# A cross-network kernel on one core: another order of the first loads and shifts, and another way to add up the last eight samples

## The chip, the cores and the metric

The kernel runs on one core of one Trainium2 chip. The metric is the device time of one execution in microseconds (us). Before the change the median of three runs is 484.85 us (484.78 to 485.05). Profiled times below are counted from the start of the profiled span, which is 482.9 us long.

## The reference

For 1024 samples, each of F = 64 fields with E = 16 values, three "cross" layers are computed. Each multiplies every field of x with every row of the layer's input h, value by value over e, and mixes the 64 x (rows of h) products to 128 outputs. Of the first two layers one half of the outputs goes to the result and the other half is the next h.

```python
x0 = x; h = x; xs = []
for i in range(3):
    z = jnp.einsum('bfe,bge->bfge', x0, h)          # products of pairs
    z = z.reshape(Bn, f0 * fh, e)
    y = jnp.einsum('oc,bce->boe', Ws[i], z) + bs[i][None, :, None]
    if i != 2:
        x_i, h = y[:, :64, :], y[:, 64:, :]
    else:
        x_i, h = y, y
    xs.append(x_i)
pooled = jnp.sum(jnp.concatenate(xs, axis=1), axis=2)   # sum over e
return pooled @ fc_w.T + fc_b                            # one number for each sample
```

As only a weighted sum over the outputs is wanted, the kernel folds the last layers into a quadratic form: what is left at the end is, for each sample, a sum over 128 rows and over e of products `uu`, and a constant.

## The kernel before

Samples are worked on in 32 chunks of 32; a chunk has N = 32 * 16 = 512 columns. `xa` holds a chunk's fields on 128 partitions (partition p is field p mod 64, so both halves of the rows hold the same data) in four slices, each turned by one field. `xb` holds four other turns. For most chunks both are loaded; for the first two chunks (numbers 2 and 3, called c0 and c1) the turns are made by matmuls with a shift matrix[...]. VectorE (and for some pieces GpSimd) makes the products `z`, TensorE contracts them with `w_all`.

The start: dummy matmuls, the constants' load on ACT's queue, the first loads on SP's queue, the first shifts.

```python
    vs = const_tile("vs", [128, NV])
    nc.scalar.dma_start(out=vs, in_=vec)
    ...
    fv2 = const_tile("fv2", [128, 32])
    nc.scalar.copy(fv2, fc2.to_broadcast([128, 32]))      # fc2 is a column of vs
    ...
    misc = ps.tile([128, N], F32, tag="acc", name="misc", bufs=4)
    zeros = nc.const_aps.tensor(0.0, [128, 128])
    for n in (128,) * 6 + (64,):
        nc.tensor.matmul(misc[:, 0:n], zeros, zeros[:, 0:n], start=True, stop=True)
    ...  # load_xa, load_xb
    c0, c1, c2, c3 = HEAD                                 # 2, 3, 0, 1
    load_xa(c0, slice(0, 1))
    nc.sync.dma_start(out=w0t[:, 0, :], in_=wh)           # weight block 0
    load_xa(c0, slice(1, 2))
    load_xa(c0, slice(2, 4))
    load_xa(c1, slice(0, 1))
    nc.sync.dma_start(out=w0t[:, 1:NJ, :], in_=w0r)       # weight blocks 1 to 3
    load_xa(c1, slice(1, 4))
    ...
    def shift_pair(c, js):
        for r, j in enumerate(js):                        # shift j reads rows halves[r]
            for h in range(2):
                at = 4 * (j + 1) + 16 * h
                nc.tensor.matmul(
                    xbs[c][j][halves[h]], shift[halves[r], at : at + F],
                    xas[c][halves[r], 0, :], start=True, stop=True,
                )

    for j, tag in enumerate(("y", "y", "set", "acc")):
        shifted(c0, j, tag)                               # takes a PSUM buffer of that tag
    shift_pair(c0, (0, 1))
    shift_pair(c0, (2, 3))
```

The first chunk's products and contraction. `h1_weights(j)` adds the two halves of weight block j on VectorE; one half is copied to PSUM by ACT first. The products of shift 1 are GpSimd's, from a copy that ACT makes, as is product 3 of c1.

```python
    nc.scalar.copy(w0o[0], w0s[0][:, :, 1, :])
    h1_weights(0, w0o[0])
    nc.scalar.copy(xb_gps[:, 0, :], xbs[c0][1])
    xbs[c0][1] = xb_gps[:, 0, :]
    for i in ((0, 2), (2, 3), (3, 4)):
        product(c0, 1, *i, engine=nc.gpsimd)
    product(c0, 0, 0, 1)
    product(c0, 0, 1, 2)
    product(c0, 0, 2, NI)
    nc.scalar.copy(w0o[1], w0s[1][:, :, 1, :])
    product(c0, 2, 0, 2)
    h1_weights(1, w0o[1])
    product(c0, 2, 2, NI)
    ...  # the same for weight blocks 2 and 3
    half_contract(c0, 0)

    for j, tag in ((0, "y"), (3, "acc"), (1, "y"), (2, "set")):
        shifted(c1, j, tag)
    shift_pair(c1, (0, 3))
    half_contract(c0, 1)
    shift_pair(c1, (1, 2))
    ...
    product(c0, 3)
    load_chunk(c3)
    half_contract(c0, 2, 3, last=3)
```

Later, `head_q` contracts the same products with further weights (the q part), which go through DRAM (`md`, read back as `ms`) and are added on VectorE.

The end. The last chunk is contracted in two pieces: 24 samples, then the last 8 (`CUT` is 24). `factors` makes `uu` of a piece (ACT copies one factor, VectorE multiplies), `sums` adds it up over e on VectorE, `pool` over the rows with a matmul whose weights are ones, and `finish` adds the constant `cst` and stores.

```python
    first, last = slice(0, CUT), slice(CUT, CB)
    factors(NCH - 1)
    sums(NP - 1, slice(64, 128), slice(0, 1), first)
    for j in range(NJ):
        contract(NCH - 1, j, 1)
    factors(NCH - 1, slice(1, 2))
    sums(NP - 1, slice(64, 128), slice(0, 1), last)
    pool(NP - 1, NP, start=False, stop=True)
    finish(NP - 1, NP, nc.sync, nc.vector)
```

Of the kernel before, what the change touches and what calls it, by code (L numbers as in the profile page):

```python
# [37 lines left out]
F32 = mybir.dt.float32  # L38
AF = mybir.ActivationFunctionType
ALU = mybir.AluOpType  # L40
AX = mybir.AxisListType

F = 64
E = 16
B = 1024
CB = 32
N = CB * E
H2 = N // 2
CUT = 24
NCH = B // CB  # L50
NI = 4
NJ = 4
NT = NI * NJ
XR = 128 + NI
# [10 lines left out]
def cin_kernel(ctx, tc, xra, xrb, wh, w0r, w1h, w2t, wx1, wx0, vec, out):  # L65
    nc = tc.nc
# [6 lines left out]
    ps = ctx.enter_context(tc.tile_pool(name="ps", bufs=2, space=bass.MemoryType.PSUM))  # L73
    dr = ctx.enter_context(tc.tile_pool(name="dr", bufs=1, space=bass.MemoryType.DRAM))
    halves = [slice(0, F), slice(F, 128)]

    def const_tile(name, shape):
        return const.tile(shape, F32, tag=name, name=name)
# [10 lines left out]


    vs = const_tile("vs", [128, NV])
    nc.scalar.dma_start(out=vs, in_=vec)
    fc2, bh1, bh2 = vs[:, 0:1], vs[:, 1:2], vs[0:64, 2:3]
    bcol, fcol, fcb = vs[:, 3:5], vs[:, 5:7], vs[:, 7:8]
    w0ds, fcr = vs[:, 8:72], vs[:, 72:200]

    fv2 = const_tile("fv2", [128, 32])
    nc.scalar.copy(fv2, fc2.to_broadcast([128, 32]))

    v0w = const_tile("v0w", [128, 2, F])  # L100
    v1w = const_tile("v1w", [128, 2, F])
# [2 lines left out]


    zeros = nc.const_aps.tensor(0.0, [128, 128])
    for n in (128,) * 6 + (64,):
        nc.tensor.matmul(misc[:, 0:n], zeros, zeros[:, 0:n], start=True, stop=True)  # L108

    shift = const_tile("shift", [128, 96])  # L110
# [1 line left out]
    for base in (0, 64, -64):  # L112
        nc.gpsimd.affine_select(
            out=shift, in_=shift, compare_op=ALU.not_equal, fill=1.0, base=base,
# [3 lines left out]
    ones = const_tile("ones", [128, 2])  # L118
# [9 lines left out]
    res = const_tile("res", [128, 128])  # L128


    xas, xbs, xxs, xrs, sqs = {}, {}, {}, {}, {}

    def load_xa(c, at=slice(0, NI)):
        if c not in xas or at.start == 0:
            xas[c] = xp.tile([128, NI, N], F32, tag="xa", name=f"xa_{c}")
        nc.sync.dma_start(
            out=xas[c][:, at, :],
            in_=bass.AP(
                tensor=xra.tensor, offset=c * XR * N + at.start * N,
                ap=[[N, 128], [1, (at.stop - at.start) * N]],  # L140
            ),
        )

# [25 lines left out]
    def load_chunk(c):  # L169
        load_xa(c)  # L170
        load_xb(c)

    c0, c1, c2, c3 = HEAD
    w0t = z_tile("w0t")
    w2s = [flat_tile(f"w2_{k}") for k in range(2)]
    w1s = set_tile("w1s")
    load_xa(c0, slice(0, 1))
    nc.sync.dma_start(out=w0t[:, 0, :], in_=wh)
    load_xa(c0, slice(1, 2))
    load_xa(c0, slice(2, 4))  # L180
    load_xa(c1, slice(0, 1))
    nc.sync.dma_start(out=w0t[:, 1:NJ, :], in_=w0r)
    load_xa(c1, slice(1, 4))
    w0s = [w0t[:, j, :].rearrange("p (i v g) -> p i v g", v=2, g=F) for j in range(NJ)]
    xb_gps = xp.tile([128, NJ, N], F32, tag="xb", name="xb_gps")
# [14 lines left out]
    def shift_pair(c, js):  # L200
        for r, j in enumerate(js):
# [4 lines that stand above are left out]
                    xas[c][halves[r], 0, :], start=True, stop=True,  # L206
                )

    for j, tag in enumerate(("y", "y", "set", "acc")):
        shifted(c0, j, tag)  # L210
    shift_pair(c0, (0, 1))
    shift_pair(c0, (2, 3))
# [2 lines left out]
    acc = const_tile("acc", [128, 2, NCH // 2, CB])  # L215
    hb = const_tile("hb", [128, NF // 2, N])
    accs, uus, zs, ys, parts = {}, {}, {}, {}, {}
# [26 lines left out]
    def tiles(j):  # L244

        return (1, 2, 3, 0) if j == NJ - 1 else range(NI)
# [42 lines left out]
                    )  # L289


    def half_contract(c, *js, last=None):
        for j in js:
            for i in tiles(j):
                t = j * NI + i
                for n in range(2):
                    nc.tensor.matmul(  # L297
                        accs[c][halves[n]], w_all[:, t, 0:64],
                        zs[c, j][:, i, n * H2 : (n + 1) * H2],
                        start=(t == 0), stop=(j == last and i == tiles(j)[-1]),  # L300
                    )
# [42 lines left out]
    def sums(k, rows=slice(0, 128), of=slice(0, 2), half=slice(0, CB)):  # L344

        nc.vector.tensor_reduce(  # L346
            acc[rows, of, k, half],
            uus[k][rows, of, E * half.start : E * half.stop].rearrange("p k (b e) -> p k b e", e=E),
            AX.X,
            ALU.add,  # L350
        )
# [27 lines left out]
    nc.vector.memset(w0o[3][SQ, 0, :], 0.0)  # L379
    for j in (2, 3):  # L380
        h1_weights(j, w0o[j])
    half_contract(c0, 0)


    for j, tag in ((0, "y"), (3, "acc"), (1, "y"), (2, "set")):
        shifted(c1, j, tag)
    shift_pair(c1, (0, 3))
    half_contract(c0, 1)
    shift_pair(c1, (1, 2))
    new_acc(c1, H2)  # L390
# [2 lines left out]

    product(c0, 3)
    load_chunk(c3)
    half_contract(c0, 2, 3, last=3)
    keep_h1(c0)

# [8 lines left out]
    for n in range(2):  # L407
        pv = ps.tile([128, 512], F32, tag=("set", "y")[n], name=f"pv2_{n}")
        for k in range(4):
            nc.tensor.matmul(  # L410
                pv[32 * k : 32 * k + 32], fv2, w2s[n][:, k * 512 : (k + 1) * 512],
                start=True, stop=True,
# [6 lines left out]
    for h in range(2):  # L419
        at = slice(32 * h, 32 * h + 32)  # L420
# [40 lines left out]
    for half, queue in enumerate((nc.sync, nc.scalar)):  # L461
        queue.dma_start(
            out=m_ap(0, 32 * half, [[row, F], [1, 32 * F]]), in_=m_rows[halves[half]]
# [86 lines left out]
        head_q(0, j)  # L550

    cst = const_tile("cst", [128, 1])
    made = set()

    def load_products(c, other=None):
# [46 lines left out]
    NP = NCH // 2  # L602
    QP = NP // 4
# [7 lines left out]
            tile_position=(0, 32 * g), skip_group_check=True, **flags,  # L611
        )

    def finish(k0, k1, queue, engine=nc.scalar):
        g, at = k0 // QP, slice(k0 % QP, (k1 - 1) % QP + 1)
        rows = slice(32 * g, 32 * g + 2)
        if engine is nc.scalar:
            engine.activation(res[rows, at, :], po[rows, at, :], AF.Identity, bias=cst[rows])
        else:
            engine.tensor_scalar(res[rows, at, :], po[rows, at, :], cst[rows], None, ALU.add)  # L620
        queue.dma_start(out=outs[:, k0:k1, :], in_=res[rows, at, :])


# [1 line left out]
    for s, c in enumerate(order):  # L625
        k, head = c // 2, c in HEAD
        if order[s - 1] in HEAD and not head:
            for n in range(NF // 2):
                x_v0x(n)
            for n in HEAD:  # L630
                factors(n)
                if n % 2:
                    sums(n // 2)
        if 0 < s < len(order) - 2 and s not in (2, 3):
            load_products(*order[s + 2 : s + (4 if s == 6 else 3)])
        if s in (2, 3):

            if s == 2:
                for n in order[4:6]:
                    load_chunk(n)  # L640
                load_shared(0)
            for j in (0, 1) if s == 2 else (2, 3):
                for n in order[4:6]:
                    product(n, j)
        if s == len(HEAD) + 5:

            pc = ps.tile([128, 1], F32, tag="set", name="pc")
            for j in range(2):
                nc.tensor.matmul(  # L649
                    pc, fcol[:, j : j + 1].to_broadcast([128, 128]), bcol[:, j : j + 1],  # L650
                    start=(j == 0), stop=(j == 1),
                )
            nc.scalar.activation(cst, pc, AF.Identity, bias=fcb, scale=float(E))
        if not head:
            if c % 4 < 2:
                new_acc(c)
            if c == NCH - 1:
                factors(c - 1)
                sums(k, of=slice(1, 2))
                sums(k, slice(0, 64), slice(0, 1))  # L660
                done = acc[:, :, 0:k, :]
                nc.vector.tensor_tensor(done[:, 0], done[:, 0], done[:, 1], ALU.add)
                po = ps.tile([128, QP, CB], F32, tag="set", name="po")
            for j in range(NJ):
                contract(c, j)
                if c == NCH - 1 and j == 1:
                    quarters = [(n, min(n + QP, k)) for n in range(0, NP, QP)]
                    for at in quarters:
                        pool(*at, start=True, stop=True)
                    pool(k, NP, 1, start=True, stop=False)  # L670
                    for at in quarters:
                        finish(*at, nc.sync)
        elif c % 2:
            for n in (c - 1, c):
                new_acc(n)
            for j in range(NJ):
                head_q(k, j)
            contract_shared(0)
        if c % 4 == 1 and not head:
            for n in (1, 2):  # L680
                new_acc(c + n)
            contract_shared(c - 1)
        if s == 0:
            v0_weights()
            load_products(order[2], order[3])

        if c == HEAD[0] or c % 4 in (0, 3) and s and order[s - 1] not in HEAD and c < NCH - 1:
            factors(order[s - 1])
            if order[s - 1] % 2:
                sums(order[s - 1] // 2)  # L690
        elif c % 4 == 2 and not head:
            factors(c - 2)
            factors(c - 1)
            x_v0x(k - 1)
            x_v0x(k)
            sums(k - 1)


    first, last = slice(0, CUT), slice(CUT, CB)
    factors(NCH - 1)  # L700
    sums(NP - 1, slice(64, 128), slice(0, 1), first)
    for j in range(NJ):
        contract(NCH - 1, j, 1)
    factors(NCH - 1, slice(1, 2))
    sums(NP - 1, slice(64, 128), slice(0, 1), last)
    pool(NP - 1, NP, start=False, stop=True)
    finish(NP - 1, NP, nc.sync, nc.vector)


# [69 lines left out]
```

## Time and profile before

| what | value |
|---|---|
| median time | 484.85 us |
| profiled span | 482.9 us |
| TensorE clock granted over the span, mean | 1.0 |
| VectorE busy | 369.0 us (76%) |
| GpSimd busy | 15.4 us (3%) |
| data moved | 87.01 MB, mean 180 GB/s |
| TensorE, main contraction (L256) | 387.6 us |
| TensorE, shifts (L204) | 32 records, 3.9 to 12.9 us |
| first store of the result / last store issued | 470.8 / 480.9 us |

In the profile PE is TensorE's matmul side and PEld its weight loads, DVE is VectorE, ACT ScalarE, POOL GpSimd, SP the engine that issues most DMAs. An fp32 matmul leaves two records. A line such as "9.52 0.38 ACT L373 COPY w0p<-w0t" says: start and length in us, engine, source line, operation, written tile and read tile; the bracket after it has the idle time of the engine before it and what ended that. The end of a matmul is modelled, so its start is the better mark.

### The profile page before, as it was taken

To read this page: it belongs to the slowest core of one execution; us is meant where nothing else is said; L and a number is where in the kernel's file an instruction comes from. 1 tells how busy PE (TensorE), PEld (TensorE's weight loads), DVE (VectorE), ACT (ScalarE), POOL (GpSimd) and SP (SyncE) were. 2 spreads that over 40 slices of the span, in tenths; PEclk is the share of its full clock that TensorE was granted. 3 is DMA by queue.
4 is the path that set the end of the run, shared out by engine and by line. 5 is a ranking of instruction groups with operands and counts; after the bars stand their busy time and mean duration, and the time that the engine had idled before them with its cause. 6 is when DMAs were issued, how large, how long until landed. Compare 5 with 4: busy or idle time off the path is not lost.

```text
span 482.9 us, 4412 instructions
## 1 busy us (share of the span) xinstructions
PE 478.2 (99%) x1802; PEld 215.3 (45%) x1802; DVE 369.0 (76%) x228; ACT 66.9 (14%) x141; POOL 15.4 (3%) x16
## 2 busy tenths in 40 slices
PE   8999999999999999999999999999999999999997
PEld 5564344443344444444444444444444444444555
DVE  5993799998899988898877686766878677771321
ACT  3242033011110121002100011001000010000001
POOL 5330000000000000000000000000000000000000
PEclk9999999999999999999999999999999999999999
DMA  8986996662952683587247344473346630000000
GB/s 336 402 277 185 388 375 276 222 213 113 347 233 91 230 281 119 187 271 281 109 159 219 145 174 175 158 212 111 128 174 215 220 138 38 0 1 0 0 1 1
DMA packets 19658, 87.01 MB, mean 180 GB/s; under 512 B 4818, under 2 KB 5490, under 8 KB 10742
## 3 DMA queue, kind: packets, MB, share of 16 engines
q1 hardware_dynamic: 18582, 85.71, 49.0%
q10 hardware_dynamic: 1056, 1.02, 0.8%
q8 instruction: 14, 0.23, 0.2%
q14 instruction: 6, 0.05, 0.0%
HBM read 85.08 MB, written 1.64 MB: 180 GB/s over the span
## 4 chain that ended last, share of the span: by engine, by line
PE 99%; DVE 1%; issue 0%; ACT 0%
PE acc L256 80%; PE acc L297 6%; PE acc L315 6%; PE acc L272 3%; PE acc L285 1%; PE xp L204 1%; PE misc L108 1%; DVE z L234 1%; PE pm L434 0%; PE pv L410 0%; PE y L277 0%; PE po L609 0%; DVE uu L337 0%; PE pc L649 0%; DVE acc L346 0%
## 5 line engine op out<-in xcount | busy, mean ns | idle before, releaser
L256 PE MATMUL acc<-z,w_all 128*128 128x512 f32 (+2 forms) x928 | 387.6, 579 | 0.0
L234 DVE TENSOR_TENSOR z<-xa,xb 128x2048 f32<-128x2048 f32 x124 | 278.4, 2286 | 41.6 <-PE acc L256 35.3
L256 PEld LDWEIGHTS acc<-z,w_all 128*128 128x128 f32 x928 | 173.1, 190 | 213.0 <-issue 205.9
L239 ACT ACTIVATE z<-xa 32x512 f32<-32x512 f32 x34 | 21.3, 626 | 337.5 <-DVE z L234 335.8
L337 DVE SCALAR_TENSOR_TENSOR uu<-acc,vs,q 64x512 f32<-64x512 f32 (+2 forms) x29 | 21.2, 731 | 57.8 <-ACT q L331 57.6
L297 PE MATMUL acc<-z,w_all 128*64 128x256 f32 x256 | 29.1, 382 | 0.5 <-DVE z L234 0.5
L315 PE MATMUL acc<-z,w_all 128*64 128x512 f32 x128 | 27.9, 593 | 0.0
L331 ACT COPY q<-acc 64x512 f32<-64x512 f32 (+2 forms) x33 | 18.7, 566 | 35.9 <-PE acc L256 19.8
L297 PEld LDWEIGHTS acc<-z,w_all 128*64 128x64 f32 x256 | 18.0, 137 | 12.7 <-DVE z L234 2.1
L234 DVE TENSOR_TENSOR z<-xa,xp 128x2048 f32<-128x2048 f32 (+2 forms) x12 | 20.3, 1746 | 0.6 <-PE xp L204 0.6
L346 DVE TENSOR_REDUCE acc<-uu 128x64 f32<-128x1024 f32 (+4 forms) x19 | 20.3, 1073 | 0.3
L315 PEld LDWEIGHTS acc<-z,w_all 128*64 128x64 f32 x128 | 9.1, 137 | 18.0 <-issue 17.1
L277 PE MATMUL y<-xr,v0w 32*64 32x512 f32 x128 | 15.9, 600 | 0.0
L272 PE MATMUL acc<-xr,v1w 32*64 32x512 f32 (+2 forms) x132 | 15.7, 587 | 0.0
L342 DVE SCALAR_TENSOR_TENSOR uu<-y,cx,xx 128x512 f32<-128x512 f32 x16 | 11.3, 746 | 0.2
L234 POOL TENSOR_TENSOR z<-xa,xb_gps 128x512 f32<-128x512 f32 (+2 forms) x4 | 9.4, 2376 | 4.4 <-ACT xb_gps L366 4.4
L272 PEld LDWEIGHTS acc<-xr,v1w 32*64 32x64 f32 x132 | 5.1, 131 | 10.0 <-issue 9.8
L285 PE MATMUL acc<-sq,w_sq 32*64 32x512 f32 (+2 forms) x132 | 8.7, 574 | 0.0
L533 DVE TENSOR_TENSOR w_all<-ms 128x256 f32<-128x256 f32 x4 | 1.6, 423 | 5.1 <-DMA ms<-md 5.1
L167 ACT ACTIVATE sq<-xr 128x512 f32<-128x512 f32 x8 | 5.0, 630 | 3.2 <-DMA xr<-in_xra 3.0
L285 PEld LDWEIGHTS acc<-sq,w_sq 32*64 32x64 f32 x132 | 3.7, 132 | 3.7 <-issue 3.5
L234 POOL TENSOR_TENSOR z<-xa,xb 128x2048 f32<-128x2048 f32 x1 | 4.6, 4584 | 13.4 <-DMA xb<-in_xrb 13.4
(57 smaller groups left out, 67.6 us busy)
## 6 DMA issues: line engine op xcount, KB each, us to landing
xa<-in_xra SPq DMA_DIRECT2D x32, 1024.0 KB, 4.9
xb<-in_xrb SPq DMA_DIRECT2D x31, 1024.0 KB, 7.7
xr<-in_xra SPq DMA_DIRECT2D x32, 128.0 KB, 7.5
xx<-in_xra SPq DMA_DIRECT2D x32, 128.0 KB, 7.6
w<-in_w2t SPq DMA_DIRECT2D x2, 1024.0 KB, 10.7
w1s<-in_w1h SPq DMA_DIRECT2D x1, 1024.0 KB
w1x<-in_wx SPq DMA_DIRECT2D x1, 1024.0 KB
w0x<-in_wx SPq DMA_DIRECT2D x1, 1024.0 KB, 5.5
```

Source lines behind the costliest of these rows:

```text
L234: engine.tensor_tensor(zs[c, j][:, at, :], xas[c][:, at, :], xbs[c][j].unsqueeze(1).to_broadcast([128, last - first, N]), ALU.mult,)
L239: nc.scalar.activation(zs[c, j][SQ, 0, :], xas[c][SQ, 0, :], AF.Square)
L256: nc.tensor.matmul(acc_c, w_all[:, t, w_cols(c)], zs[c, j][:, i, cols], start=(t == 0 and c % 4 < 2), stop=(t == NT - NI and c % 4 >= 2),)
L272: nc.tensor.matmul(acc_c[halves[1 - n]], v1w[at, m], xr[:, cols], start=(m == 0 and c not in ends), stop=False, tile_position=(at.start, 6 ...
L277: nc.tensor.matmul(ys[c // 2][halves[n]], v0w[at, m], xr, start=(m == 0), stop=(m == 1), tile_position=(at.start, 64 * n),)
L285: nc.tensor.matmul(acc_c[halves[n]], w_sq[at, w_cols(c)][:, 64 * n : 64 * n + 64], sqs[first][at, cols], start=h and (first == 0 or c not ...
L297: nc.tensor.matmul(accs[c][halves[n]], w_all[:, t, 0:64], zs[c, j][:, i, n * H2 : (n + 1) * H2], start=(t == 0), stop=(j == last and i == ...
L315: nc.tensor.matmul(accs[c][halves[1 - c % 2]], w_all[:, t, 64:128], zs[c, j][:, i, :], start=(t == 0), stop=False,)
L331: nc.scalar.copy(q[h, cols], acc_c[64 - h.start : 128 - h.start])
L337: nc.vector.scalar_tensor_tensor(uu[:, cols], acc_c[h], bh1[h], q[h, cols], ALU.add, ALU.mult)
L342: nc.vector.scalar_tensor_tensor(uu_tile(k)[:, 1, :], ys[k], cx, xxs[k], ALU.add, ALU.mult)
L346: nc.vector.tensor_reduce(acc[rows, of, k, half], uus[k][rows, of, E * half.start : E * half.stop].rearrange("p k (b e) -> p k b e", e=E), ...
```

## The change

It has two parts. At the start, the first load comes in two halves of 64 rows, the constants `vs` move behind the weights on SP's queue, weight block 1 gets a load of its own, one dummy matmul goes, and the contraction of product 0 is split around the next chunk's first shifts. This is meant to let the first shifts and the first contraction steps begin when their own data is there, and to fill a wait of TensorE with shifts. At the end, the last 8 samples are added up over the 128 rows on TensorE first, the constant's share (`csl`, 1/(128 * 16) of it on each row) with them by a second matmul, and over e by one VectorE reduction from PSUM straight into the stored result. This is meant to take one VectorE step out of the last chain.

```diff
-    nc.scalar.dma_start(out=vs, in_=vec)
...
-    nc.scalar.copy(fv2, fc2.to_broadcast([128, 32]))
...
-    for n in (128,) * 6 + (64,):
+    for n in (128,) * 5 + (64,):
         nc.tensor.matmul(misc[:, 0:n], zeros, zeros[:, 0:n], start=True, stop=True)
...
-    def load_xa(c, at=slice(0, NI)):
+    def load_xa(c, at=slice(0, NI), rows=slice(0, 128)):
...
-    load_xa(c0, slice(0, 1))
+    for rows in halves:
+        load_xa(c0, slice(0, 1), rows)
     nc.sync.dma_start(out=w0t[:, 0, :], in_=wh)
     load_xa(c0, slice(1, 2))
     load_xa(c0, slice(2, 4))
     load_xa(c1, slice(0, 1))
-    nc.sync.dma_start(out=w0t[:, 1:NJ, :], in_=w0r)
+    for at in (slice(0, 1), slice(1, NJ - 1)):
+        nc.sync.dma_start(out=w0t[:, at.start + 1 : at.stop + 1, :], in_=w0r[:, at])
+    nc.sync.dma_start(out=vs, in_=vec)
     load_xa(c1, slice(1, 4))
...
-    for j, tag in enumerate(("y", "y", "set", "acc")):
+    for j, tag in ((1, "y"), (0, "y"), (2, "set"), (3, "acc")):
         shifted(c0, j, tag)
...
-    half_contract(c0, 0)
+    half_contract(c0, 0, at=(0, 1))
...
     shift_pair(c1, (0, 3))
+    half_contract(c0, 0, at=(2, 3))
     half_contract(c0, 1)
...
     load_chunk(c3)
+    nc.scalar.copy(fv2, fc2.to_broadcast([128, 32]))
     half_contract(c0, 2, 3, last=3)
...
+    csl = const_tile("csl", [128, 1])
+    nc.gpsimd.memset(acc[64:128, 0, NCH // 2 - 1, CUT:], 0.0)
...
             nc.scalar.activation(cst, pc, AF.Identity, bias=fcb, scale=float(E))
+            nc.scalar.activation(csl, cst, AF.Identity, scale=1.0 / (128 * E))
...
-    first, last = slice(0, CUT), slice(CUT, CB)
+    first, last = slice(0, CUT), slice(E * CUT, N)
     factors(NCH - 1)
     sums(NP - 1, slice(64, 128), slice(0, 1), first)
     for j in range(NJ):
         contract(NCH - 1, j, 1)
     factors(NCH - 1, slice(1, 2))
-    sums(NP - 1, slice(64, 128), slice(0, 1), last)
     pool(NP - 1, NP, start=False, stop=True)
-    finish(NP - 1, NP, nc.sync, nc.vector)
+    pl = ps.tile([1, N - E * CUT], F32, tag="acc", name="pl", bufs=4)
+    uu = uus[NP - 1]
+    nc.tensor.matmul(pl, ones[:, 1:2], uu[:, 1, last], start=True, stop=False)
+    nc.tensor.matmul(
+        pl, csl, nc.const_aps.tensor(1.0, [128, N - E * CUT]), start=False, stop=False
+    )
+    nc.tensor.matmul(pl, ones[:, 1:2], uu[:, 0, last], start=False, stop=True)
+    rows, (even, odd) = slice(96, 98), (outs[0:1, NP - 1], outs[1:2, NP - 1])
+    nc.scalar.activation(
+        res[rows, QP - 1], po[rows, QP - 1], AF.Identity, bias=cst[rows]
+    )
+    nc.sync.dma_start(out=even, in_=res[96:97, QP - 1])
+    nc.sync.dma_start(out=odd[:, first], in_=res[97:98, QP - 1, first])
+    rl = hb[0:1, 0, 0 : CB - CUT]
+    nc.vector.tensor_reduce(rl, pl.rearrange("p (b e) -> p b e", e=E), AX.X, ALU.add)
+    nc.sync.dma_start(out=odd[:, CUT:], in_=rl)
```

## The prediction

> **What bounds the kernel now.** I read the page first (busy times, slices, the chain that ended last), then the chain of waits at both ends of the run, then the timeline of the first 13 us, the DMA issues of the first microsecond, and transfer rates by stage.
>
> The page's busy times:
>
> ```profile
> PE 478.2 (99%) x1802; PEld 215.3 (45%) x1802; DVE 369.0 (76%) x228; ACT 66.9 (14%) x141; POOL 15.4 (3%) x16
> ```
>
> TensorE is busy 99% of the span, and the chain is 99% PE. Neither the middle's loads nor VectorE can give much; the change touches only the first 13 us and the last 4. The chain of waits at the start (start us, us, what):
>
> ```profile
> 0.79 3.22 PE misc L108 x14
> 4.00 1.87 PE xp L204 x8
> 5.87 0.02 issue
> 5.90 2.42 DVE z L234 x3
> 8.32 0.04 issue
> 8.37 1.08 PE acc L297 x8
> 9.45 1.02 PE xp L204 x8
> ```
>
> Dummy matmuls (`misc`), first shifts (`xp`), three VectorE products, half the first contraction, the next chunk's shifts. At 5.90 to 8.32 PE waits on VectorE: a contraction step of two 128x256 matmul pairs is 0.43 us (1.08 us for 8 records, less the tail), so of 8.37 minus 7.24 (start of the second step) about 0.7 us is empty. How that goes on, in the timeline of 8.9 to 10.6 us:
>
> ```profile
> 6.68 4.84 POOL L234 TENSOR_TENSOR z<-xa,xb_gps 128x1024 f32<-128x1024 f32 x3 [4.42 <-ACT xb_gps L366]
> ...
> 9.52 0.38 ACT L373 COPY w0p<-w0t 128x256 f32<-128x256 f32 x1 [2.98 <-DVE z L234]
> ...
> 9.93 0.42 DVE L354 TENSOR_TENSOR w_all<-w0t,w0p 128x256 f32<-128x256 f32 x1 [0.49 <-ACT w0p L373]
> ...
> 10.46 0.23 PEld L297 LDWEIGHTS acc<-z,w_all 128*64 128x64 f32 x4 [0.88 <-POOL z L234]
> ```
>
> GpSimd makes product 1 of the first chunk in three pieces, 6.68 to 11.52. ACT copies the second weight block only at 9.52; the named releaser (`z` on DVE) is no operand of that copy, but `w0t` is, so I take it for the 768 KB load of `w0r`. The combined weights are ready at 10.35 and PE goes on at 10.46. First DMA issues, KB, median us to landing:
>
> ```profile
> xa<-in_xra SPq DMA_DIRECT2D x1, 256.0 KB, 3.0
> vs<-in_vec ACTq DMA_DIRECT2D x1, 100.0 KB, 3.2
> ```
>
> xa is issued at 0.74, lands near 3.79, and the first shift starts at 3.94: the load ends last there, not the dummies, whose last record starts at 3.58. Two 1 us windows (busy per engine, clock, DMA share, GB/s), with loads of 128 rows and then loads of 64 and 32 rows under way:
>
> ```profile
> 3.40:4.40 1.00, 1.00 (x8) 0.72 (x10) 0.00 (x0) 0.22 (x1) 0.00 (x0) 1.00 1.06 408
> 61.00:62.00 1.00, 1.00 (x3) 0.38 (x2) 1.00 (x1) 0.16 (x1) 0.00 (x0) 1.00 0.86 213
> ```
>
> A load of fewer rows runs at about half the rate. The end, in the timeline:
>
> ```profile
> 479.55 0.36 DVE L337 SCALAR_TENSOR_TENSOR uu<-acc,vs,q 64x128 f32<-64x128 f32 x1 [2.15 <-ACT q L331]
> 479.94 0.28 DVE L346 TENSOR_REDUCE acc<-uu 64x8 f32<-64x128 f32 x1
> 480.34 0.12 PEld L609 LDWEIGHTS po<-acc,ones 128*2 128x2 f32 x2 [1.31 <-ACT q L331]
> 480.37 0.22 PE L609 MATMUL po<-acc,ones 128*2 128x32 f32 x2 [1.15 <-DVE acc L346]
> 480.63 0.26 DVE L620 TENSOR_SCALAR res<-po,cst 2x32 f32<-2x32 f32 x1 [0.40 <-PE po L609]
> 480.92 0.25 SPq L621 DMA_DIRECT2D out<-res  x1
> ```
>
> A serial tail: product, sum over e, sum over rows, add the constant, store.
>
> **What the Trainium skill says.** "TensorE: Matmul & The Clock Gate", Part 1: the array starts at half clock and is released after a busy window of about 3.4 us, which is free-running, so the moment varies. The trace agrees: eight shift records take 1.75 us from 3.94 (two groups of four, 0.85 us each), and the next eight 0.86 us from 5.68. "SBUF — State Buffer", Door 1: 64 partitions reach only 8 of 16 DMA ports, half the rate; 213 against 408 GB/s above agrees. "DMA: Bandwidth & Descriptors", Anatomy of one DMA: a fixed cost near 2 us, mostly completion; so halving a load cannot halve its 3.0 us. "VectorE: DVE Perf Modes", errata section: an fp32 tensor_tensor takes (N+151)/0.96 ns; for N = 512 that is 691, the trace has 684. The fixed part means a reduction of 128 values (0.28 us here) hardly depends on how many rows it has.
>
> **The change, part by part.**
>
> *One dummy fewer.* The last of the records starts at 3.58, after 6.25 units of 128 columns: about 0.45 us each. PE is free at about 3.26 instead of 3.7. It is worth nothing alone, as the load lands at 3.79.
>
> *First load in two halves, `vs` later.* Before, 262 KB of xa and 102 KB of vs interleave: at 400 GB/s 0.91 us. The first half is 131 KB at 213 GB/s, 0.62 us, so it lands about 0.3 to 0.4 earlier, 3.45. Shift 0 reads only this half: start 3.45 + 0.14 = 3.6, end 1.75 later (cold) at 5.35, product on VectorE at 5.35 + 0.22 (before, 5.68 to 5.90) = 5.55 or so instead of 5.90: gain 0.35. (The first weights, ready at 5.26 before, allow that.) The second half is issued 0.48 us later and its 0.62 us follows the first's: I expect 3.85, as late as all of xa before. Shift 1 reads it and feeds ACT's copy and GpSimd, so GpSimd gains 0.05, perhaps 0.3 if the halves overlap.
>
> *Half of contraction 0 before the next chunk's shifts, half after; other order of the two y buffers.* The shifts (0.86 us and two gaps of 0.14) move into the 0.7 us hole, and their y buffer comes from ACT's early copy. PE finishes contraction 0 and shifts at about 9.4 instead of 10.3. xa of the next chunk has to be there by 7.5; it has 1.57 MB with what comes before it, at 400 GB/s from 2.6 on 6.6, plus 0.4: 7.0.
>
> *`w0r` in two loads.* The second block alone ends at 1.83 MB, about 7.7 instead of some 9.5. The combination no longer waits 0.49 us for ACT; VectorE does it after its 0.35 earlier products, at 9.05, ready at 9.45 instead of 10.35. So contraction 1 could start at 9.55 instead of 10.49.
>
> *What then ends last: GpSimd.* Its third piece is done at 11.52 less 0.05 to 0.3; the last step takes 0.1 latency and 0.43: contraction 1 ends at 11.75 to 12.0 instead of 12.24. PE has been handed 0.9 us there and waits for most of it. Front gain 0.2 to 0.5, I take 0.3.
>
> *Does it stay?* TensorE has no other hole up to 41.7 us. The tightest later point is the second weight block of the q part: its VectorE addition ends at 44.05, PE wants it at 41.70 + 16 records of 0.215 = 45.1: slack 1.05. The first product after that waits for xb until 51.6 and is done at 53.9, wanted at 55.5: slack 1.6. A gain of 0.3 fits in both even if these loads don't move.
>
> *The tail.* Removed: reduction 0.28 plus 0.03, the 0.22 us row sum, the add 0.26. Added after the product (ends 479.91): a row sum of 128 columns. Start 0.15 later as before, 480.06; second record 0.11 later, 0.275 long: 480.45. Then a reduction of 1x128 from PSUM, 0.03 later, 0.28 to 0.34 long: 480.79. Store at 480.82 instead of 480.92: gain 0.1. The two other stores are issued after ACT's 0.3 us activation at about 479.9 and 480.2, so the SP queue is free by 480.5. The constant's matmul and the memset lie off the path.
>
> Sum: 0.3 + 0.1 = 0.4, so 484.85 - 0.4 = 484.45 us.
>
> **Rivals.**
> *The GpSimd wait does not take over*, since its pieces start earlier than I think: contraction 1 then ends up to 1.0 earlier, 483.75. For it: both halves may well land early, since they go to different rows and can overlap. Against: 10.46's releaser is GpSimd already, and half-rate loads.
> *The clock is released later*, since there is less dummy work or a gap before the shifts. One window later costs up to 3.4/2 = 1.7 us on PE, part of it hidden behind VectorE: about 485.8. Against: the gap stays near 0.3 us, and before had 0.25. Chance 5%.
> *The early gain is swallowed by a transfer in the middle* (q weights or xb): only if the slacks 1.05 and 1.6 shrank. 484.75, the tail alone.
> *The tail turns worse*: three small stores end instead of one, each in pieces of a few bytes; if the landing grows by 0.2, the tail loses 0.1: 484.65.
>
> **Range and chances.** The main uncertainty is the second half's landing (0.3 us of the result), then the tail (0.15 either way), then the clock. 80% range: 483.9 to 484.9. Nothing here reaches 9.7 us, 2%, so: faster 0.01, within 2% 0.98, slower 0.01.
>
> **What would show it.** Right: `xp` starts near 3.6; the VectorE product near 5.55 while ACT's `xb_gps` copy stays near 5.9; the next chunk's shifts near 7.5; the `w_all` addition ends near 9.45; PE then waits for GpSimd, with its third piece near 11.4; q contraction starts at 41.4; the last store 0.9 us after the last `uu`. Wrong: GpSimd starting before 6.4 (gain up to 1), cold shifts beyond 6.0 (clock), or a wait on `ms` or `xb` in front of a contraction at 41 to 56 us.

## The result and the profile after

The changed kernel takes 486.15 us (median of 6 runs, 485.72 to 487.2) against 484.95 us of the kernel before (6 runs, 484.61 to 485.31). The ratio is 1.0028 with a 95% interval of 1.0015 to 1.0041: slower by about 1.2 us, where 0.4 us faster was predicted. The profiled execution took 486.88 us, at the slow end of the six, so its excess over the first profile of before is larger than the median's.

The page's busy times of the changed kernel, to be held against those of before:

```profile
PE 479.8 (99%) x1806; PEld 215.5 (44%) x1806; DVE 368.7 (76%) x227; ACT 67.5 (14%) x143; POOL 15.5 (3%) x17
```

They tell nearly nothing: TensorE is 99% busy again. The loss sits where TensorE waits. The waits of its first 22 us (who waited for what: us in total, times, longest):

```profile
ACT w0p L374 <- DMA w0t<-in_w0r: 3.3, 1, 3.3
...
DVE z L235 <- DMA xa<-in_xra: 1.9, 1, 1.9
...
PE xp L205 <- DMA xa<-in_xra: 1.1, 1, 1.1
...
PE pv L413 <- DMA w<-in_w2t: 0.8, 1, 0.8
```

The last three waited for no transfer before. The first, ACT's copy of weight block 1, waited before too (until 9.52); it now waits until 10.33, although its block has become a load of its own. SP's timeline of the first 8 us of the changed kernel (start, length, issue) shows how the queue got there:

```profile
0.74 1.21 SPq L134 DMA_DIRECT2D xa<-in_xra  x2
2.00 0.59 SPq L177 DMA_DIRECT2D w0t<-in_wh  x1
2.63 1.37 SPq L134 DMA_DIRECT2D xa<-in_xra  x3
4.05 0.91 SPq L182 DMA_DIRECT2D w0t<-in_w0r  x2
5.00 0.43 SPq L183 DMA_DIRECT2D vs<-in_vec  x1
5.47 0.86 SPq L134 DMA_DIRECT2D xa<-in_xra  x1
6.38 1.36 SPq L188 DMA_DIRECT2D w<-in_w2t  x2
```

In the same view of before, wh is issued at 1.22, w0r at 3.10 and w2 from 4.05 on:

```profile
0.74 0.41 SPq L136 DMA_DIRECT2D xa<-in_xra  x1
1.22 0.41 SPq L178 DMA_DIRECT2D w0t<-in_wh  x1
1.68 1.37 SPq L136 DMA_DIRECT2D xa<-in_xra  x3
3.10 0.43 SPq L182 DMA_DIRECT2D w0t<-in_w0r  x1
3.57 0.43 SPq L136 DMA_DIRECT2D xa<-in_xra  x1
4.05 1.20 SPq L187 DMA_DIRECT2D w<-in_w2t  x2
```

The two half loads take 1.21 us to issue, where one whole load took 0.41; the issue of wh behind them takes 0.59 instead of 0.41. So wh is issued 0.78 us later and w0r 0.95. The loads of w2 are 2.3 us later, but 1.2 to 1.3 of that is there with a whole first load too (they are issued from 5.38 and 5.20 on in whole_load and whole_six_again, below), where the second load of w0r and vs stand ahead of them. What moved in the first 8 us is the last column, in GB/s, of one window over 0 to 8 us, first in before and then in the changed kernel:

```profile
0.00:8.00 8.00, 7.10 (x38) 4.15 (x38) 2.52 (x4) 2.46 (x4) 2.75 (x12) 1.00 0.77 286
```

```profile
0.00:8.00 8.00, 7.22 (x32) 4.06 (x34) 1.62 (x3) 2.25 (x3) 2.29 (x12) 1.00 0.64 188
```

That is 286 x 8 us = 2.29 MB against 1.50 MB: 0.79 MB behind, and at the 420 GB/s of later stretches some 1.9 us. The last consumer of that backlog is the matmul on the second w2 load (timeline of 17 to 21 us; the bracket has the idle time and what ended it):

```profile
18.29 1.06 PE L413 MATMUL pv<-w,fv 128*32 128x512 f32 x8
...
20.18 1.07 PE L413 MATMUL pv<-w,fv 128*32 128x512 f32 x8 [0.83 <-DMA w<-in_w2t]
```

Before, all 16 records ran in one piece from 17.00, the second half from 17.88, and the second load had landed by 16.2:

```profile
17.00 1.92 PE L410 MATMUL pv<-w,fv 128*32 128x512 f32 x16
```

The q contraction starts at 44.03 instead of 41.70 (first the line of before, then that of the changed kernel):

```profile
41.70 13.90 PE L315 MATMUL acc<-z,w_all 128*64 128x512 f32 x64
```

```profile
44.03 13.90 PE L316 MATMUL acc<-z,w_all 128*64 128x512 f32 x64
```

That is 2.3 us lost in front of it, as much as the spans differ (485.1 - 482.9 = 2.2). From there on nothing is lost.

The tail ran in the expected order (timeline):

```profile
481.88 0.36 DVE L338 SCALAR_TENSOR_TENSOR uu<-acc,vs,q 64x128 f32<-64x128 f32 x1 [2.15 <-ACT q L332]
...
482.29 0.38 PE L718 MATMUL pl<-uu,ones 128*1 128x128 f32 x2 [0.20 <-DVE uu L338]
...
482.71 0.28 DVE L726 TENSOR_REDUCE hb<-pl 1x8 f32<-1x128 f32 x1 [0.47 <-PE pl L718]
483.01 0.23 SPq L727 DMA_DIRECT2D out<-hb  x1
```

From the start of the last product to the last store's issue it is 483.01 - 481.88 = 1.13 us, before 480.92 - 479.55 = 1.37 us. From that issue to the end of the span it is 485.10 - 483.01 = 2.09 us, before 482.88 - 480.92 = 1.96 us, so of the 0.24 us gained 0.13 go again.

### The profile page after: what moved, and what is told of

Read it like the earlier page. It is cut to its first block, busy times and chain, and to the rows that moved or that the text cites. A ratio compares the mean times of both kernels' runs of the same rounds, so it can differ in the third digit from the quotient of the medians.

```text
span 485.1 us, 4428 instructions
## 1 busy us (share of the span) xinstructions
PE 479.8 (99%) x1806; PEld 215.5 (44%) x1806; DVE 368.7 (76%) x227; ACT 67.5 (14%) x143; POOL 15.5 (3%) x17
## 4 chain that ended last, share of the span: by engine, by line
PE 95%; DMA 3%; SPq 1%; issue 0%; DVE 0%; ACT 0%
PE acc L257 80%; PE acc L316 6%; PE acc L298 4%; PE acc L273 3%; DMA w<-in_w2t 3%; PE acc L286 1%; SPq L134 1%; PE pm L437 0%; PE y L278 0%; PE pv L413 0%; SPq L182 0%; SPq L188 0%; SPq L177 0%; SPq L183 0%; PE pl L718 0%
## 5 line engine op out<-in xcount | busy, mean ns | idle before, releaser
L347 DVE TENSOR_REDUCE acc<-uu 128x64 f32<-128x1024 f32 (+3 forms) x18 | 20.0, 1117 | 0.3
L205 PE MATMUL xp<-xa,shift 64*64 64x512 f32 x32 | 6.3, 815 | 1.1 <-DMA xa<-in_xra 1.1
```

The lines of the kernel that those rows point to most:

```text
L347: nc.vector.tensor_reduce(acc[rows, of, k, half], uus[k][rows, of, E * half.start : E * half.stop].rearrange("p k (b e) -> p k b e", e=E), ...
```

## The experiments

All compare with the kernel before on the same chip in the same series; there, before had medians of 485.55 to 485.91 us, about 0.8 us above the first measurement, so only differences within a series are used. Four theories stood against each other: the half loads hold up all transfers behind them (transfer); one dummy matmul fewer lets the clock be released later (clock); the order of vs and of the weight loads (order); the small stores at the end (tail).

### First series: one part at a time

**tail_only**: before with the new tail (and `csl` and the memset).

> The kernel before with the new tail alone. Start theory (all of the loss arises before the contraction of the q part begins): the tail gains what the profile of after shows, 0.1 us from the last uu to the last store's completion, so 484.7 to 485.0, ratio 0.9995 to 1.0001, and the q contraction starts at 41.7 as before. Tail theory (the three small stores cost): 0.3 us or more slower.

Measured: 485.55 us against 485.81, ratio 0.9999 (0.9991 to 1.0006). The tail costs nothing; in these times a gain of 0.1 us cannot be told from none. In the profile the q contraction starts at 44.19 instead of 41.7, as TensorE ran at half clock for a stretch at 10.6 us (taken up below).

**start_only**: the changed kernel with the old tail.

> The changed kernel with the old tail. Start theory: as slow as the changed kernel or 0.1 us slower, ratio to before 1.002 to 1.004. Tail theory: back at 484.9.

Measured: 486.05 us against 485.81, ratio 1.0008 (1.0000 to 1.0017). In the profile the q contraction starts at 43.06. The size is below the expected range, but the loss is in the start and not in the tail.

**whole_load**: the changed kernel with

```diff
-    for rows in halves:
-        load_xa(c0, slice(0, 1), rows)
+    load_xa(c0, slice(0, 1))
```

> The changed kernel, but the first load of xa in one piece of 128 rows. Transfer theory (two loads of 64 rows start late and run at half rate, and everything behind them on the queue is later): first shift near 3.8, w2 landed before 17.5 and no wait for it, and the kernel is no slower than before, 484.3 to 484.9. Clock theory (one dummy fewer lets the clock be released one window later): still 485.5 to 486.5. Order theory (vs and the split weight load behind it hold up the queue): still w2 after 19 and slower than before.

Measured: 485.32 us against 485.81, ratio 0.9997 (0.9989 to 1.0005); q starts at 41.92. It is not slower than before; the first shift starts at 3.69. But the second w2 matmul still waits 0.57 us for its load and starts at 18.07, where no wait was expected. So one part of the order theory holds: the changed order of the loads brings w2 late by itself.

**halves_only**: the same edit the other way round, in before.

> The kernel before with the first load of xa in two halves and nothing else. Transfer theory: first packets near 2.1 us instead of 1.7, w2 lands 1 us or more later than at 16.2, and the kernel is 0.5 to 1.3 us slower than before. Clock and order theories: within 0.3 us of before.

Measured: 488.30 us against 485.81, ratio 1.0055 (1.0043 to 1.0067), only 5 runs. More than any theory had said. In its profile two things add up. The transfers are late (1.56 MB by 8 us), so TensorE has next to nothing to do. TensorE's timeline:

```profile
6.72 1.25 PE L298 MATMUL acc<-z,w_all 128*64 128x256 f32 x8
11.07 1.66 PE L298 MATMUL acc<-z,w_all 128*64 128x256 f32 x8 [3.09 <-DVE z L235]
12.65 1.99 PE L205 MATMUL xp<-xa,shift 64*64 64x512 f32 x8
```

And then its clock is taken back. Two windows of 3.41 us (busy per engine PE, PEld, DVE, ACT, POOL; granted clock; DMA share; GB/s):

```profile
8.02:11.43 3.41, 0.36 (x4) 0.29 (x6) 1.64 (x2) 0.00 (x0) 2.54 (x3) 1.00 1.01 402
11.43:14.85 3.42, 3.42 (x18) 0.88 (x16) 2.72 (x5) 1.18 (x4) 0.91 (x1) 0.50 1.02 429
```

A window with 0.36 us of matmuls in 3.41 is followed by one at half clock: the shifts take 1.99 us instead of 1.09.

### Second series: what about the halves costs

**column_halves**: before, with the first load cut by columns, so each part has 128 rows.

```diff
-    load_xa(c0, slice(0, 1))
+    for cols in (slice(0, H2), slice(H2, N)):
+        load_xa(c0, slice(0, 1), cols)
```

> The kernel before with the first load of xa cut in two by columns (each 128 rows, 256 columns of 4 bytes), so as many loads and bytes as with two halves of 64 rows. If the 64 rows are what costs (issue time, half rate, what follows): issues of 0.41 us as before, 1.9 MB or more moved by 8 us, and a time within 0.5 us of before. If one more load at the head of the queue costs: 1.5 MB by 8 us and 1.5 to 2.5 us slower than before, as with the halves.

Measured: 486.40 us against 485.70, ratio 1.0007 (0.9996 to 1.0019), runs from 485.17 to 487.84. The issues take 0.41 us, as expected for the 64-row theory, but 1.48 MB by 8 us, as expected for the other. By time it cannot be settled. Without the runs that had a window at half clock (sorted as in the fourth series) its 12 runs have a median of 486.14 against 485.68 of 35 runs of before; the 0.5 us between them are as much as the halves of 64 rows cost there, but the 12 runs spread from 485.17 to 486.81.

**halves_two_queues**: before, with the halves of 64 rows on two queues.

```diff
-    load_xa(c0, slice(0, 1))
+    for rows, queue in zip(halves, (nc.sync, nc.scalar)):
+        load_xa(c0, slice(0, 1), rows, queue)      # vs follows on nc.scalar
```

> The kernel before with the two halves of 64 rows issued side by side, the first on SP's queue, the second on ACT's queue ahead of vs. If SP's longer issue of a 64-row load and the delay of what comes behind it cost the time: wh is issued 0.6 us earlier than with both halves on SP, and half or more of the 2.5 us comes back. If the load of 64 rows itself upsets the transfers: 1.6 MB by 8 us again and 1.5 us or more slower than before.

Measured: 485.81 us against 485.70, ratio 0.9997 (0.9987 to 1.0007); wh is issued at 1.37, 1.94 MB by 8 us. The same loads of 64 rows show no cost once they do not stand one behind the other at the head of SP's queue, though each still takes 0.57 to 0.60 us to issue. This takes away two things at once: wh no longer waits for a second issue, and the two halves move side by side (264 and 301 GB/s at 2 to 3 and 3 to 4 us, against 164 and 205 in the changed kernel).

**whole_seven**: whole_load with `(128,) * 6` dummies.

> The changed kernel with the first load whole and the seventh dummy matmul back. Clock theory: the clock is released no later and never taken back, and the kernel is 0.2 us or more faster than with six dummies, which had ratio 0.9997. Transfer theory: the first shift waits for the load anyway, so the dummy changes nothing, ratio 0.999 to 1.000.

Measured: 485.03 us against 485.70, ratio 0.9985 (0.9977 to 0.9992). Faster than before, by more than whole_load was; whether that is the dummy the next series was to tell.

**before_again**: before, a second profile.

> The kernel before once more, for a second profile of the same program. If the slow stretch of the transfers between 4 and 8 us and the moment of the clock's release belong to the program, both are as in the first profile: 2.3 MB by 8 us, release at 5.7 us. If they vary from run to run: another moment of release, and less moved by 8 us, with a later q contraction (41.7 us before) by as much as the time differs.

Measured: 485.74 us; the clock is released at 6.70 instead of 5.65, 1.93 MB by 8 us instead of 2.29, q starts at 42.79 instead of 41.70. So the first profile of before was a lucky one. In before_again the transfers have a slow stretch too, just a shorter one than in the changed kernel. (The clock's column reads 1.00 before the release as well; the release is read from where the record of the clock begins.) Windows of 1 us in before_again:

```profile
4.00:5.00 1.00, 1.00 (x9) 0.40 (x12) 0.15 (x1) 0.38 (x1) 0.00 (x0) 1.00 1.30 254
5.00:6.00 1.00, 1.00 (x12) 0.34 (x8) 0.31 (x2) 0.00 (x0) 0.00 (x0) 1.00 0.76 227
6.00:7.00 1.00, 1.00 (x8) 0.00 (x0) 0.93 (x2) 0.58 (x1) 0.14 (x1) 1.00 1.00 391
```

and in the changed kernel:

```profile
5.00:6.00 1.00, 1.00 (x8) 0.26 (x4) 0.57 (x2) 0.38 (x1) 0.00 (x0) 1.00 1.18 225
6.00:7.00 1.00, 1.00 (x8) 0.23 (x2) 1.00 (x2) 0.59 (x1) 0.00 (x0) 1.00 0.89 244
7.00:8.00 1.00, 1.00 (x10) 0.34 (x6) 0.05 (x1) 0.00 (x0) 0.87 (x1) 1.00 0.83 266
```

Two slow microseconds there, three here, on top of a slow one at 3 to 4 us (205 GB/s, where only the half loads and the first of wh were under way).

### Third series: halves and dummies, two by two, on one chip

**after_again** (the changed kernel), **after_seven** (with `(128,) * 6`), **whole_six_again** (first load whole), **whole_seven_again** (both).

> The changed kernel itself, beside three variants of it on one chip. Transfer theory: 0.5 us or more slower than with the first load whole, 1.5 to 1.6 MB by 8 us; against before on this chip 0.1 to 0.3% slower.

> The changed kernel with the seventh dummy back, halves kept. Clock theory: 0.4 us or more faster than with six. Transfer theory: within 0.3 us of the changed kernel.

> The changed kernel with the first load whole, six dummies. Transfer theory: 0.5 us or more faster than the changed kernel, 0.3 to 0.6 us faster than before. Clock theory: no faster than the changed kernel.

> First load whole and seven dummies. Clock theory: 0.4 us or more faster than with the load whole and six dummies. Transfer theory: within 0.3 us of it, and 0.5 to 0.8 us faster than before.

| first load | six dummies | seven dummies |
|---|---|---|
| two halves | 485.95 us, 1.0010 (1.0001 to 1.0020) | 485.76 us, 1.0010 (0.9999 to 1.0022) |
| whole | 484.86 us, 0.9989 (0.9982 to 0.9996) | 485.35 us, 0.9993 (0.9984 to 1.0002) |

Before: 485.55 us. The halves cost 1.1 us with six dummies and 0.4 with seven, on average 0.75 us. The dummy's two differences have opposite signs (-0.2 and +0.5): no effect that these runs show. The clock theory falls for the changed kernel. With the first load whole, the rest of the change is faster than before, by 0.11% here. The same kernel, as whole_load, had 0.9997 (0.9989 to 1.0005) in the first series; all four measurements with a whole first load lie below 1, two of them with their whole interval. So this version is faster than the changed kernel, and ahead of before by about 0.1% at most.

Against before the changed kernel is only 0.4 us slower here (485.95 - 485.55), where the first measurement had 1.2 us. The other 0.8 us is the difference between before then (484.95) and before in the four series (485.55 to 485.91); the changed kernel itself hardly moved (486.15, 485.95). Why before was faster then stays open.

### Fourth series: what remained open

**halves_again**: halves_only once more.

> The two half loads alone in the kernel before, again. If late transfers take the clock back: 2 to 3 us slower than before again, a clock record with a second half-speed window of 3.4 us within the first 15 us, and TensorE idle for over 1.5 us between 8 and 13 us. If that was chance: 0.5 to 1.2 us slower and one release.

Measured: 486.69 us against 485.91, ratio 1.0021 (1.0010 to 1.0032), 22 runs up to 488.83. In the profile the clock is released once (5.22) and stays. Of each run the mean granted clock is known, and one window at half clock (1.7 us of 485) must lower that mean from 1.000 to about 0.9965. The runs fall apart accordingly, into those at 0.998 or more and those at 0.995 to 0.996:

| kernel | runs at 0.998 or more | median, us | runs at 0.996 or less | median, us |
|---|---|---|---|---|
| before, first series | 34 | 485.79 | 1 | 487.54 |
| halves_only | 0 | | 5 | 488.30 |
| before, fourth series | 43 | 485.86 | 8 | 487.49 |
| halves_again | 14 | 486.38 | 8 | 488.35 |

So the 2.5 us of halves_only are two things, of which only the first is in every run: the halves themselves, 0.5 us (486.38 - 485.86) or 0.8 us (488.30 - 487.54), and a window at half clock, 1.6 to 2.0 us. It was taken back in 13 of 27 runs of these halves, in 15 of 181 runs of before over the four series, and in none of 79 runs of the kernels with the change's start and six dummies (halves or whole). The 1.2 us of the changed kernel hold none of it. Why five runs of five had it in the first series, and 8 of 22 later, stays open.

**order_only**: before with the split contraction, the other order of the y buffers, and weight block 1 loaded by itself.

> The kernel before with the contraction of product 0 split around the next chunk's shifts, the other order of the y buffers and weight block 1 as a load of its own; first load, vs, dummies and tail as before. If these hold the gain: 0.4 to 0.7 us faster than before, contraction 1 starts near 10.2 us. If vs holds it: within 0.2 us of before.

Measured: 485.71 us against 485.91, ratio 0.9995 (0.9987 to 1.0003). Contraction 1 starts at 10.76 (11.58 in before_again), but the second w2 matmul waits 0.51 us for its load, and the time shows no sure gain.

**vs_only**: before with vs on SP's queue behind the weights, its copy behind product 3.

> The kernel before with vs moved behind the weights on SP's queue and its copy behind product 3. If vs in the first load's way costs time: first load landed 0.2 us earlier and 0.2 to 0.4 us faster than before. If the order holds the gain: within 0.2 us of before.

Measured: 485.45 us against 485.91, ratio 0.9988 (0.9979 to 0.9997): the only single part with an interval below 1, by 0.0003; among sixteen intervals that may be chance. The first load landed at 3.49 instead of 3.79 (profile), but the first shift still starts at 3.93, behind the seven dummies.

**after_two_queues**: the changed kernel with the second half on ACT's queue.

> The changed kernel with the second half of the first load on ACT's queue. If SP's issue time is what the halves cost: wh is issued near 1.4 instead of 2.0 us, and most of the 0.8 us comes back, 0.4 us or more faster than before. If loads of 64 rows themselves cost: as slow as the changed kernel, 0.3 us or more slower than before.

Measured: 485.73 us against 485.91, ratio 0.9998 (0.9990 to 1.0006); wh is issued early again (1.37), q starts at 42.87. The loss against before is gone, so at least a part of the halves' cost has come back (a whole first load had 0.9989 and 0.9997 with six dummies), but the gain of 0.4 us has not come.

Seven of the eighteen profiles side by side (one execution each, so single rows carry chance; times in us):

| kernel | first shift | MB by 8 us | contraction 1 starts | w2 matmuls start | q starts | time |
|---|---|---|---|---|---|---|
| whole_seven | 3.93 | 2.16 | 10.20 | 16.83, 17.72 | 41.54 | 484.36 |
| before | 3.94 | 2.29 | 10.49 | 17.00, 17.88 | 41.70 | 484.67 |
| whole_six_again | 3.69 | 2.06 | 9.65 | 16.50, 18.27 | 42.12 | 484.92 |
| before_again | 3.93 | 1.93 | 11.58 | 18.08, 18.96 | 42.79 | 485.74 |
| after_again | 3.51 | 1.55 | 11.55 | 18.05, 19.56 | 43.41 | 486.29 |
| after | 3.51 | 1.50 | 11.79 | 18.29, 20.18 | 44.03 | 486.88 |
| halves_only | 3.93 | 1.56 | 14.57 | 21.19, 22.07 | 45.90 | 488.79 |

Time minus q start is between 442.8 and 443.0 in all of them: the middle and the tail are the same for all within 0.2 us, and the time is decided in the first 20 us. The two kernels with the earliest first shift (3.51) are slower than the four with a whole first load.

Taken over all profiles, MB by 8 us parts the kernels cleanly: 1.50 to 1.82, mean 1.62, in the six with both halves on SP's queue, and 1.92 to 2.29, mean 2.05, in the nine with a whole first load. At 420 GB/s the 0.43 MB between the means are 1.0 us, about what the later issue (0.78 to 0.95 us) comes to. With the halves on two queues it is 1.94 and 1.70 MB and with the load cut by columns 1.48, so these three don't sort by that issue alone. The 0.79 MB of the first two profiles were a small value against the largest one.

## Why the prediction was wrong, point by point

*What bounds the kernel.* Half right. The sum of the start and a constant rest holds, and the q weights and xb took back nothing. But I called the start a chain of PE and VectorE with data arriving in time. It hangs on the transfers' progress over the first 8 us.

*The load ends last at 3.94, not the dummies.* Wrong, a coincidence of 0.1 us. With seven dummies the first shift starts at 3.93 also where its load lands much earlier (the whole load at 3.49 in vs_only, the first half at 3.32 in halves_two_queues), with six and halves at 3.51, with six and a whole load at 3.69. A dummy is worth 0.43 us there, which is lost later.

*First load in two halves.* This is the step that failed. Its term was "gain 0.35" for VectorE's first product and 0.05 to 0.3 for GpSimd. In the changed kernel's timeline of 0 to 20 us:

```profile
4.39 0.29 PEld L205 LDWEIGHTS xp<-xa,shift 64*64 64x64 f32 x6 [0.59 <-DMA xa<-in_xra]
5.02 0.38 ACT L365 COPY w0p<-w0t 128x256 f32<-128x256 f32 x1 [2.99 <-DMA w0t<-in_wh]
...
5.77 1.28 DVE L235 TENSOR_TENSOR z<-xa,xp 128x512 f32<-128x512 f32 x2
...
6.41 0.59 ACT L367 COPY xb_gps<-xp 128x512 f32<-128x512 f32 x1 [1.01 <-PE xp L205]
7.13 4.83 POOL L235 TENSOR_TENSOR z<-xa,xb_gps 128x1024 f32<-128x1024 f32 x3 [4.88 <-ACT xb_gps L367]
```

The first shift was as early as forecast (3.51). But the second half was issued 0.65 us after the first and not 0.48, and the shift that reads it waited until 4.39, where 3.85 was forecast for its landing: ACT's copy comes at 6.41 instead of 5.95 and GpSimd starts at 7.13 instead of 6.68, so 0.45 us were lost there. And "the first weights, ready at 5.26 before, allow that" no longer held: wh, behind the halves, came later, its copy waited for it until 5.02, the weights were ready at 5.85, and the product began at 5.77 instead of 5.55, a gain of 0.13. The sum went no further. Left out was what the halves do to everything else behind them on the queue: wh issued 0.78 later and w0r 0.95 later, so that the third product waited 1.91 us and the next chunk's shifts 1.05 us for their loads. In the two by two of halves and dummies (third series) the halves cost 1.1 and 0.4 us, 0.75 on average.

That the cost comes from two loads one behind the other at the head of SP's queue is what halves_two_queues and after_two_queues support. What of that pair costs is not shown. The half rate of loads into 64 rows, as the prediction took it, does fit the changed kernel (205 GB/s at 3 to 4 us, with the DMA engines busy 0.61 of the time), but on two queues the halves moved side by side at more than that, so these two runs take away the half rate together with the later issue. The fixed cost near 2 us, which the prediction took from "DMA: Bandwidth & Descriptors" of the Trainium skill, Anatomy of one DMA, stands there for transfers issued by GpSimd; these loads are issued by SP, and the first half landed 2.6 us after its issue (halves_two_queues), the whole load 3.0 us.

*Split contraction and separate weight load.* The mechanism is right where the loads are in time. Timeline of whole_six_again:

```profile
7.63 1.09 PE L204 MATMUL xp<-xa,shift 64*64 64x512 f32 x8
...
9.09 0.41 DVE L354 TENSOR_TENSOR w_all<-w0t,w0p 128x256 f32<-128x256 f32 x1
...
11.30 0.20 PEld L297 LDWEIGHTS acc<-z,w_all 128*64 128x64 f32 x4 [0.58 <-POOL z L234]
```

Shifts at 7.63 (predicted 7.5), the addition done at 9.50 (9.45), then the wait for GpSimd's third piece (11.24, predicted near 11.4). In the changed kernel these were 9.71, 11.65 and 11.96, the first two right behind a transfer that they waited for.

*Does it stay?* The list of later consumers was incomplete. I checked the q weights at 45 us and xb at 51, not the w2 matmul at 17.9 (its load landed at 16.2, slack 1.7). In the changed kernel it waits 0.83 us for that load, and with a whole first load still 0.57 (whole_load): the new order of the loads puts w2 further back by itself. In whole_six_again the same matmul waits too, there for a VectorE product (0.70 us), so part of an early gain is given back at 18 us.

*The tail.* Predicted 0.1 us. The profile has 0.24 us up to the last store's issue and loses 0.13 behind it: the rival of a longer landing came true in part, and 0.1 remains. The time of tail_only cannot confirm it (0.9999, 0.9991 to 1.0006), but the profiles do: time minus q start is 442.84 us on average in the nine with the new tail (442.77 to 442.93) and 442.93 in the nine with the old one (442.89 to 443.00).

*The rivals.* The clock was given 5% and 1.4 us, on the ground of less dummy work. In the two by two the dummy shows no effect. But the clock is taken back when transfers are so late that TensorE has little to do for a window; seen in halves_only, and in tail_only at 10.6 us after 1.58 us of matmuls in 3.41. It threatens before's start (15 of 181 runs), while none of the 79 runs with the change's start and six dummies had it. The range 483.9 to 484.9 was too narrow already because of before: its runs in the series lay between 484.3 and 486.3 even without a half-clock window, and its medians at 485.6 to 485.9, which one median of three runs did not show. The rival that came true, a transfer *made late by the change*, was not on the list; I asked only whether transfers hide the gain.

## What to carry to other kernels

Cutting a first load so that its consumer starts sooner can make every load behind it on that queue later; here it did, by 0.8 us. Before doing it, follow the queue to its last consumer with small slack, here the matmul at 17.9 us, and leave the load whole (the faster choice here) or issue the extra part on another queue, which here only took the loss away. Also take the spread of the kernel before from more than one profile, when the expected gain is below its spread.

## What the runs showed of the hardware

- A first load of 64 rows of 2 KB takes 0.57 to 0.60 us to issue on SP or ACT, one of 128 rows in its place 0.41. The order of sizes was not expected. The number of rows alone does not set it: wh, with 128 rows, takes 0.41 behind the whole load and 0.57 to 0.59 behind a half.
- In 15 of the 18 profiles at least one microsecond between 3 and 8 us moves less than 300 GB/s (down to 156), where 420 are moved later; the length differs for the same program (none in the first profile of before, two such microseconds in before_again). Its cause is open; no run here controls it.
- The clock's release lies anywhere from 3.8 to 7.1 us in these profiles, with six or seven dummies. Its taking back lasts exactly one window: half clock from 10.61 to 14.03 in tail_only and from 11.44 to 14.85 in halves_only. "TensorE: Matmul & The Clock Gate" of the Trainium skill, Part 1, gives a free-running window of 3413 ns, and both stretches agree with it. The windows ahead of them held 1.58 and 0.36 us of matmuls in 3.41; windows with 2.02 us (column_halves, from 7.75) and 2.10 us (halves_again, from 8.63) were not followed by half clock.
